# A gated cross-attention and routed-expert kernel: order of the first batches, paced products on GpSimd, and where rows are turned

## The chip, the core and the metric

The kernel runs on one core of one Trainium2 chip. The metric is device time in microseconds (us) of that core, the median of several runs. Engines are called as in the profile: PE (TensorE, with PEld for its weight loads), DVE (VectorE), ACT (ScalarE), POOL (GpSimd) and SP (SyncE, which here only issues transfers). Each runs its own instructions in program order and waits on semaphores for the others.

## The reference

All values are float32. There are 16 batches of 128 rows of 128 features (x) and 77 context rows of 96 features each.

```python
def _layernorm(x, axis=-1, eps=1e-05): ...
# cross-attention: 16 heads of 8
q = (x @ Wq.T + bq).reshape(b, l, h, dh)
kv = (y @ Wkv.T + bkv).reshape(b, m, h, 2 * dh)
k, v = kv[..., :dh], kv[..., dh:]
att = softmax(einsum('blhd,bmhd->blmh', q, k) / sqrt(dh), axis=2)
out = einsum('blmh,bmhd->blhd', att, v).reshape(b, l, d) @ Wo.T + bo
# experts: 4 rounds, 4 experts of 512 hidden features, the best 2 of each row
for r in range(4):
    logits = flat @ Wg[r] + bg[r]
    vals, idx = top_k(logits, 2);  w = softmax(vals)
    cw = sum(one_hot(idx, 4) * w)
    y = einsum('enf,efh->enh', gelu(flat @ W1 + b1), W2) + b2
    cur = cur + einsum('ne,enh->nh', cw, y)
# the whole
x = x + tanh(g_xattn) * xattn(_layernorm(x), ctx)
x = x + tanh(g_ffn) * ffn(_layernorm(x))
```

## The kernel before

**Attention.** The 16 batches are taken one after the other (loop at L1027, "step b"), in four blocks of four. For a block, x is normalized (`stats_x`, `norm_x`, class `Norm` at L236: statistics on DVE, the power -0.5 on POOL at L252, the application on DVE or POOL), turned by PE (`turn_x`), projected to queries (`queries`); the context is turned (`turn_ctx`), and projected to keys and values. `spread_keys` (L744, POOL) multiplies a batch's keys with a mask of heads, so that `scores` (four products into two double banks) gives all heads. `weights` takes the maximum and the difference on DVE and the exponential on ACT; `turn_weights` transposes the exponentials on PE and copies them back on ACT; `attend` sums them and weighs the values on PE, divides on DVE (L820, L822); `put_out` projects. In step b, PE turns the exponentials of b and computes the scores of b+1 in between.

What else has to be done is hung on the steps by hand: the lists `early[b]`, `extra[b]` and `behind[b]` (L908 to L975) hold the turning and projecting of later blocks, the constants of the routing, the gate of the first half and its stores. The order of PE, DVE, ACT and POOL is exactly this program order.

**Start.** SP loads blocks of x and context in turns (L141), ACT's queue the weights (L128 to L133), POOL's queue two bias rows (L137). PE fills its waits with products of a zero tile (`warm`, L664), nine, two, ten, three and four of them. All four batches of the first block are normalized, turned and projected (L844 to L859) before the first scores (L861); the constant rows (`spread_rows`, L867) follow the first exponentials.

**Experts.** The rows are split in two halves h of 1024. In four rounds each half is routed: `gate` ranks the logits, `count`, `route` and `places` find for each row a place, `scatter` (POOL, indirect DMA) stores the rows sorted by their pair of experts into DRAM, `load` (SP) fetches them, `turn_half` transposes them on PE. A phase p (L1111; half p % 2, round p // 2) works through 21 units: eight tiles, five borders, eight tiles. A unit is `first_layer` (four pairs of PE instructions, then gelu on ACT) and, one unit later, `second_layer` (PE, then a sum into the rows on DVE, L1090). `bring` (L991) copies a tile's expert weights on DVE four units ahead (L1000). While one half is in the experts, the other is routed, by the lists `mid[i]` and `post[i]` of the phase.

From round 1 on the logits come without PE: `multiply` (L406, POOL) multiplies the rows with the gate's weights into one of four buffers lp, `sum_up` (L414, DVE) reduces. The products of tiles 0 and 1 are issued in unit 13, 2 and 3 in unit 14, and so on (L1229); each waits for its rows and a free buffer. The last one is issued in unit 0 of the next phase, where also `gate` (unit 1) and `count` (after the first layer of unit 4) stand. In the last round `finish` (L1092) scales a tile and POOL stores it to the output.

**Into the experts.** The first half's stores hang on steps 11 to 14 (L973), its load is issued after step 14 (L1058). After the last step, `turn_half` for the first tiles stands between two groups of four zero products (L1274).

## Time and profile before

| | us |
|---|---|
| median of three runs (467.44 to 468.66) | 467.48 |
| the profiled execution, its own time | 467.39 |
| its span, first to last instruction | 465.6 |
| first scores of batch 0 (sc, L262) start | 18.18 |
| attention product of batch 0 (ps_av) ends | 31.07 |
| first expert product (ps_h) starts | 124.74 |
| PE's last stage (ps_y) ends about | 455.8 |
| last store of the output starts | 457.05 |

How to read it: the page gives busy time by engine, in 40 slices, by group of instructions, and the chain of waits that ended last; the trace behind it can be asked for a timeline, for waits, and for a table of busy time by stage. PEclk is the clock that PE was granted, as a share of full speed. One matmul in float32 shows as two instructions, so four products of a half layer are "x8", 0.89 us apart from start to start at full clock. A wait's cause is the engine or transfer that signalled last. Idle time of an engine that is not the bound costs nothing.

### The profile page before, as it was taken

What the parts mean: (1) busy time and instruction counts of PE and PEld (TensorE: products, weight loads), DVE (VectorE), ACT (ScalarE), POOL (GpSimd) and SP (SyncE); (2) the same over time, 40 slices, a digit from 0 to 9 for tenths busy, and PEclk for the clock granted to TensorE, in tenths of its full rate; (3) what the DMA queues carried; (4) which work ended last, traced back from release to release, by engine and by line L of the source; (5) the groups of instructions that cost most, each with busy time, mean ns of one, the idle gap of its engine ahead of it and who ended that gap; (6) DMA issues with size and microseconds to landing.
All of it is one profiled execution on the core that took longest, in us unless ns stands there. A gap on an engine that the chain in (4) does not pass through costs nothing.

```text
span 465.6 us, 12218 instructions
## 1 busy us (share of the span) xinstructions
PE 445.5 (96%) x4506; PEld 415.4 (89%) x4506; DVE 347.0 (75%) x900; ACT 275.0 (59%) x853; POOL 211.2 (45%) x249
## 2 busy tenths in 40 slices
PE   7999999989899899999999999999999999999991
PEld 6778888777799899999999999999999999999991
DVE  7259998989665998688579768857976885775551
ACT  2356776666555456566656656665665666566560
POOL 5354645227204732582366258236625924461042
PEclk8779999999999989999999999999999999999997
DMA  7420000002201400230121013012101301220000
GB/s 198 137 93 2 4 1 3 2 13 84 95 2 49 139 1 2 72 118 1 48 84 59 1 70 119 1 48 77 67 3 69 118 3 49 94 86 8 1 30 17
DMA packets 19553, 24.08 MB, mean 52 GB/s; under 512 B 3940, under 2 KB 16550, under 8 KB 19366
## 3 DMA queue, kind: packets, MB, share of 16 engines
q1 hardware_dynamic: 14868, 13.41, 9.1%
q0 software_dynamic: 3648, 9.71, 5.7%
q8 instruction: 36, 0.59, 0.5%
q10 hardware_dynamic: 978, 0.18, 0.2%
q14 instruction: 23, 0.19, 0.1%
HBM read 13.58 MB, written 9.71 MB: 50 GB/s over the span
## 4 chain that ended last, share of the span: by engine, by line
PE 81%; issue 7%; DVE 5%; POOL 3%; ACT 2%; POOLq 0%; DVEq 0%; ACTq 0%
PE ps_y L262 28%; PE ps_h L262 28%; PE ps_av L262 6%; PE ps_tr L265 6%; PE sc L262 2%; POOL out_dram L1098 2%; PE ps_warm L262 2%; PE ps_c L265 2%; PE ps_b L262 2%; DVE wb L1000 1%; PE ps_pos L262 1%; PE ps_o L262 1%; ACT exT L800 1%; DVE vm L197 1%; PE ps_q L262 1%
## 5 line engine op out<-in xcount | busy, mean ns | idle before, releaser
L1076 ACT ACTIVATE hT<-ps_h,wb 128x128 f32<-128x128 f32 x512 | 146.0, 368 | 87.9 <-ACT hT L1076 55.4
L262 PE MATMUL ps_h<-curT,wb 128*128 128x128 f32 x1024 | 136.3, 277 | 1.8 <-DVE wb L1000 1.8
L262 PE MATMUL ps_y<-wb,hT 128*128 128x128 f32 x1024 | 136.7, 277 | 0.0
L262 PEld LDWEIGHTS ps_h<-curT,wb 128*128 128x128 f32 x1024 | 125.5, 193 | 2.0 <-DVE wb L1000 2.0
L262 PEld LDWEIGHTS ps_y<-wb,hT 128*128 128x128 f32 x1024 | 125.4, 193 | 0.0
L519 POOL DMA_INDIRECT sorted<-rows,pos_i x64 | 69.6, 1087 | 116.5 <-DVE start L512 61.1
L1000 DVE COPY wb<-wall 128x1028 f32 x128 | 107.5, 842 | 11.7 <-issue 4.0
L93 POOL TENSOR_TENSOR lp<-rows,wg_rows 128x512 f32<-128x512 f32 x48 | 72.5, 1535 | 38.3 <-DVE rows L1090 31.4
L1090 DVE SCALAR_TENSOR_TENSOR rows<-ps_y,pws,rows 128x128 f32<-128x128 f32 x128 | 44.3, 346 | 36.2 <-PE ps_y L262 35.9
L1076 ACT ACTIVATE hT<-ps_h,wall 128x128 f32<-128x128 f32 x160 | 45.6, 368 | 35.9 <-PE ps_h L262 33.8
L800 ACT COPY exT<-ps_tr 77x512 f32<-77x512 f32 x64 | 34.1, 581 | 17.5 <-PE ps_tr L265 17.3
L262 PEld LDWEIGHTS ps_y<-wall,hT 128*128 128x128 f32 x320 | 38.9, 192 | 6.1 <-ACT hT L1076 6.1
L262 PE MATMUL ps_y<-wall,hT 128*128 128x128 f32 x320 | 43.1, 278 | 0.0
L262 PE MATMUL ps_h<-cx,wall 128*128 128x128 f32 x320 | 42.3, 275 | 0.0
L265 PEld LDWEIGHTS ps_tr<-ident,ex 128*77 128x77 f32 x256 | 29.5, 154 | 11.1 <-ACT exT L800 8.3
L262 PEld LDWEIGHTS ps_h<-cx,wall 128*128 128x128 f32 x320 | 39.0, 192 | 0.0
L265 PE MATMUL ps_tr<-ident,ex 128*77 128x128 f32 x256 | 36.8, 289 | 1.7 <-ACT exT L800 1.7
L417 DVE TENSOR_REDUCE lg<-lp 128x4 f32<-128x512 f32 x48 | 32.4, 675 | 5.5 <-POOL lp L93 5.5
L1098 POOL DMA_INDIRECT out_dram<-res,id_i x16 | 18.4, 1151 | 37.0 <-DVE res L1095 36.4
L782 DVE TENSOR_REDUCE mx<-sc 128x8 f32<-128x616 f32 x32 | 25.4, 792 | 11.8 <-PE sc L262 11.7
L792 ACT ACTIVATE ex<-ex 128x616 f32<-128x616 f32 x32 | 23.0, 719 | 10.9 <-DVE ex L786 10.4
L1090 DVE SCALAR_TENSOR_TENSOR rows<-ps_y,pwxs,rows 128x128 f32 x40 | 13.9, 348 | 17.0 <-PE ps_y L262 16.0
(162 smaller groups left out, 463.1 us busy)
## 6 DMA issues: line engine op xcount, KB each, us to landing
rows<-sorted SPq DMA_DIRECT2D x16, 528.0 KB
x_sb<-in_x_dram SPq DMA_DIRECT2D x4, 256.0 KB
wall<-in_L_ffn_W_dram SPq DMA_DIRECT2D x1, 1024.0 KB
wall<-in_L_ffn_W_dram SPq DMA_DIRECT2D x4, 256.0 KB
wg_rows<-wg_turned SPq DMA_DIRECT2D x1, 1024.0 KB
sorted<-rows,pos_i POOLq DMA_INDIRECT x64, 2.5
ctx_sb<-in_ctx_dram SPq DMA_DIRECT2D x4, 115.5 KB
out_dram<-res,id_i POOLq DMA_INDIRECT x16, 2.4
```

The source lines that it names most:

```text
L93: return lambda *a, **kw: tc.keep_in_program_order(f(*a, **kw))
L262: nc.tensor.matmul(*args, **kw)
L265: nc.tensor.transpose(*args)
L417: nc.vector.tensor_reduce(lgs[h][:, t, :], prods.pop((h, t)), AX.X, ALU.add)
L519: ins = nc.gpsimd.indirect_dma_start(out=sorted_rows[h], out_offset=bass.IndirectOffsetOnAxis(ap=pos_i[:, t : t + 1], axis=0), in_=rows[h] ...
L782: beats.append(nc.vector.tensor_reduce(mx, sv, AX.X, ALU.max))
L792: nc.scalar.activation(eu, eu, AF.Exp, scale=1.0 / math.sqrt(DH))
L800: nc.scalar.copy(exT[:, ts(g, HG), :].rearrange("m h l -> m (h l)"), ps[:M, :])
L1000: nc.vector.tensor_copy(wb, wall[:, ds(e, 1), :].rearrange("p o n -> p (o n)"))
L1076: nc.scalar.activation(hT[:, fc, :], ps[:, ts(fc, P)], AF.Gelu_apprx_tanh, bias=wb[:, W_B + fc : W_B + fc + 1],)
L1090: return nc.vector.scalar_tensor_tensor(at, y, w, at, ALU.mult, ALU.add)
L1098: ins = nc.gpsimd.indirect_dma_start(out=out_rows, out_offset=bass.IndirectOffsetOnAxis(ap=id_i[:, t : t + 1], axis=0), in_=res, in_offset ...
```

## The change

It reorders the start, moves single operations between steps and engines, and ties POOL's products to the sums of the units:

- x of batch 0 is loaded alone, then the first context, the two bias rows (now on SP), then the other three batches; bq is loaded into a column of its own.
- Batch 0 alone is normalized, turned and projected before the first scores; the rest of its block follows. Its keys are spread by DVE. The zero products use the banks of the scores: thirteen, one, one and three; the two groups around the last `turn_half` are gone.
- The second zeroed value block and blk are cleared by POOL, after the first scores. The first copy of ACT is a copy of one element.
- The constant rows, the residual of block 0 and the normalization of block 1 hang behind step 0; `turn_x(1)` moves from step 1 to step 2; the bias columns are turned with the constant rows.
- The first half's logits are added ahead of the division of their step; the gate's tanh moves ahead of step 12's exponentials; the stores take four places in step 12 and three in step 13, and the load comes after step 13.
- `turn_half` of the first tiles and the gelu table's first use stand in step 15 ahead of `attend`.
- `multiply` of tile t is issued in unit 13 + t and waits for the sum made in that unit; reductions follow two units later, the last two in units 0 and 1 of the next phase.
- `finish` starts one unit earlier, in another order of tiles.

```diff
@@ -119,26 +119,28 @@
-    NCOL = E * NF + 1
-    cols_n = const.tile([NCOL, P], F32, name="cols_n")
+    cols_n = const.tile([E * NF, P], F32, name="cols_n")
+    bqc = const.tile([P, 1], F32, name="bqc")
...
+    nc.scalar.dma_start(bqc, bq.rearrange("(d o) -> d o", o=1))
     wg_sb = const.tile([D, R, E], F32, name="wg_sb")
...
-    nc.scalar.dma_start(cols_n[E * NF : NCOL, :], bq.rearrange("(o d) -> o d", o=1))
-    nc.scalar.dma_start(cols_n[0 : E * NF, :], b1.rearrange("e (c p) -> (e c) p", p=P))
+    nc.scalar.dma_start(cols_n, b1.rearrange("e (c p) -> (e c) p", p=P))
     bkv_v = bkv.rearrange("(o h t d) -> o t h d", o=1, t=2, d=DH)
...
+    nc.sync.dma_start(x_sb[:, 0, :], x[0])
+    nc.sync.dma_start(ctx_sb[:, 0:BB, :], ctx_768[0:BB].rearrange("b m c -> m b c"))
     for t, w in ((0, wkT), (1, wvT)):
-        gp.dma_start(
-            w[C : C + 1, :].rearrange("o (h d) -> o h d", d=DH), bkv_v[:, t]
-        )
-    for i in range(NB):
+        nc.sync.dma_start(w[C : C + 1, :].rearrange("o (h d) -> o h d", d=DH), bkv_v[:, t])
+    nc.sync.dma_start(x_sb[:, 1:BB, :], x[1:BB].rearrange("b l d -> l b d"))
+    for i in range(1, NB):
         nc.sync.dma_start(
@@ -193,8 +195,7 @@
-    for i in range(2):
-        nc.vector.memset(vm[i], 0.0)
+    nc.vector.memset(vm[0], 0.0)
@@ -208,7 +209,6 @@
-    gp.memset(blk, 0.0)
@@ -403,13 +403,14 @@
-    def multiply(h, r, t):
+    def multiply(h, r, t, behind):
...
-        gp.tensor_tensor(
+        ins = gp.tensor_tensor(
             prods[h, t], rows[h][:, t, 0:D].unsqueeze(1).to_broadcast([P, E, D]), wg_rows[:, r],
...
+        after(ins, behind, "one tile for each piece of work")
@@ -663,29 +664,30 @@
-        ps = bank("ps_warm")
+        ps = banks2("ps_warm")
         for _ in range(n):
-            mm(ps[:, :P], zero, zero, start=True, stop=True)
-    warm(9)
-    ps = bank("ps_wkv")
-    for t in range(2):
-        tp(ps[:C, ts(t, P)], wkv_n[:, t, :], ident)
-    tp(ps[:, 2 * P : 3 * P], wq_n, ident)
-    for t, w in ((0, wkT), (1, wvT)):
-        nc.vector.tensor_copy(
-            w[0:C, :].rearrange("c (h d) -> c h d", d=DH),
-            ps[:C, : 2 * D].rearrange("c (h t d) -> c t h d", t=2, d=DH)[:, t],
-        )
+            mm(ps[:, 0, :P], zero, zero, start=True, stop=True)
+    junk = const.tile([1, 1], F32, name="junk")
+    nc.scalar.copy(junk, zero[0:1, 0:1])
     wqT = const.tile([D, D], F32, name="wqT")
-    nc.scalar.copy(wqT, ps[:, 2 * P : 3 * P])
+    def turn_projections():
+        ps = bank("ps_wkv")
+        for t in range(2):
+            tp(ps[:C, ts(t, P)], wkv_n[:, t, :], ident)
+        tp(ps[:, 2 * P : 3 * P], wq_n, ident)
+        for t, w in ((0, wkT), (1, wvT)):
+            nc.vector.tensor_copy(
+                w[0:C, :].rearrange("c (h d) -> c h d", d=DH),
+                ps[:C, : 2 * D].rearrange("c (h t d) -> c t h d", t=2, d=DH)[:, t],
+            )
+        nc.scalar.copy(wqT, ps[:, 2 * P : 3 * P])
...
-    cols = const.tile([P, NCOL], F32, name="cols")
-    bqc = cols[:, E * NF : NCOL]
@@ -716,17 +718,20 @@
-    def turn_x(i):
+    def turn_x(i, lo=0, hi=BB):
...
-        for j in range(BB):
+        for j in range(lo, hi):
             tp(ps[:, ts(j, P)], row(i * BB + j, 0, D), ident)
+        at = slice(lo * P, hi * P)
         xnTs[i] = awork.tile([P, TB], F32, tag="xnT", name="xnT")
-        nc.scalar.copy(xnTs[i], ps)
-    def queries(i):
+        nc.scalar.copy(xnTs[i][:, at], ps[:, at])
+    def queries(i, lo=0, hi=BB):
         ps = bank("ps_q")
-        mm(ps, wqT, xnTs.pop(i), start=True, stop=True)
-        nc.scalar.activation(qT[i], ps, AF.Identity, bias=bqc)
+        at = slice(lo * P, hi * P)
+        mm(ps[:, at], wqT, xnTs.pop(i)[:, at], start=True, stop=True)
+        nc.scalar.activation(qT[i][:, at], ps[:, at], AF.Identity, bias=bqc)
@@ -741,10 +746,10 @@
-    def spread_keys(b):
+    def spread_keys(b, eng=gp):
...
-        gp.tensor_tensor(
+        eng.tensor_tensor(
             km,
@@ -802,7 +807,6 @@
@@ -816,6 +820,9 @@
+        return ps
+    def over_sums(ps):
         rs = awork.tile([D, L], F32, tag="rs", name="rs")
@@ -826,55 +833,61 @@
-        nc.vector.scalar_tensor_tensor(
+        beats.append(nc.vector.scalar_tensor_tensor(
             row(b, D, D), ps[:, :D], tg[:, 0:1], x_sb[:, b, :],
...
-        )
+        ))
+    warm(13)
+    first_norm, next_norm = Norm(1, "b"), Norm(BB - 1, "c")
+    first_norm.stats(0, x_sb[:, 0, :])
+    first_norm.scale()
+    turn_projections()
     turn_ctx(0)
-    warm(2)
+    warm(1)
+    next_norm.stats(0, x_sb[:, 1, :])
+    first_norm.apply(0, row(0, 0, D), x_sb[:, 0, :], nc.vector)
+    for j in range(1, BB - 1):
+        next_norm.stats(j, x_sb[:, 1 + j, :])
+    next_norm.scale()
+    turn_x(0, 0, 1)
     keys(0)
-    ps = bank("ps_cols")
-    tp(ps[:, :NCOL], cols_n, ident[:NCOL, :NCOL])
-    nc.scalar.copy(cols, ps[:, :NCOL])
-    nc.scalar.copy(
-        wall[:, :, W_B:WW], cols[:, 0 : E * NF].rearrange("p (e c) -> p e c", c=NF)
-    )
-    for j in range(BB):
-        stats_x(0, j)
-    norms[0].scale()
-    kms = {0: spread_keys(0), 1: spread_keys(1)}
+    warm(1)
+    queries(0, 0, 1)
+    warm(3)
+    kms = {0: spread_keys(0, nc.vector), 1: spread_keys(1)}
     stats_x(1, 0)
+    for j in range(1, BB):
+        next_norm.apply(j - 1, row(j, 0, D), x_sb[:, j, :], nc.vector)
     stats_x(1, 1)
-    norm_x(0, nc.vector)
-    stats_x(1, 2)
-    stats_x(1, 3)
-    norms[1].scale()
-    norm_x(1, gp)
-    load_experts()
-    warm(10)
-    turn_x(0)
-    warm(3)
-    queries(0)
-    warm(4)
     scs = scores(0, kms.pop(0))
...
+    gp.memset(vm[1], 0.0)
+    gp.memset(blk, 0.0)
+    load_experts()
+    turn_x(0, 1, BB)
+    queries(0, 1, BB)
     turn_ctx(1)
...
-    keys(1)
...
+        tp(ps[:, 32 : 32 + E * NF], cols_n, ident[: E * NF, : E * NF])
         tp(ps[:, ts(2, D)], wo_n, ident)
...
+        nc.scalar.copy(
+            wall[:, :, W_B:WW],
+            ps[:, 32 : 32 + E * NF].rearrange("p (e c) -> p e c", c=NF),
+        )
         wgT = const.tile([R * E, D], F32, name="wgT")
@@ -907,11 +920,15 @@
+    amid = {b: [] for b in range(B)}
     behind = {b: [] for b in range(B)}
...
-    spread_rows()
-    residual(0)
-    early[1] += [lambda: turn_x(1)]
+    extra[0] += [lambda: keys(1)]
+    behind[0] += [spread_rows, lambda: residual(0)]
+    for j in range(2, BB):
+        behind[0] += [lambda j=j: stats_x(1, j)]
+    behind[0] += [lambda: norms[1].scale(), lambda: norm_x(1, gp)]
+    early[2] += [lambda: turn_x(1)]
     extra[2] += [lambda: queries(1)]
@@ -919,7 +936,7 @@
-            behind[b - 4 + j] += [lambda i=i, j=j: stats_x(i, j)]
+            behind[max(b - 4 + j, 1)] += [lambda i=i, j=j: stats_x(i, j)]
         behind[b - 1] += [lambda i=i: norms[i].scale(), lambda i=i: norm_x(i, gp, (0, 1))]
@@ -945,11 +962,12 @@
-    def gate0(g):
+    def logits0_done(g):
         add_bg(0, 0, g, first["lg"])
-        if g:
-            first["gate"] = gate(0)
-            advance(first["gate"], GATE_1)
+    def gate0():
+        first["gate"] = gate(0)
+        advance(first["gate"], GATE_1)
@@ -965,12 +983,16 @@
-    behind[7] += [lambda: logits0(0), lambda: gate0(0)]
+    amid[7] += [lambda: logits0(0), lambda: logits0_done(0)]
     extra[9] += [lambda: turned0(1)]
-    behind[9] += [lambda: logits0(1), lambda: gate0(1)]
-    behind[10] += [counted0, lambda: advance(first["gate"])]
-    behind[11] += [routed0, placed0, lambda: stored0(0)]
-    stores_at = {(12, 0): 1, (12, 1): 2, (12, 2): 3, (13, 0): 4, (13, 1): 5, (13, 2): 6, (14, 0): 7}
+    amid[9] += [lambda: logits0(1), lambda: logits0_done(1)]
+    behind[9] += [gate0]
+    behind[10] += [counted0, lambda: advance(first["gate"], GATE_2 - GATE_1)]
+    extra[11] += [lambda: advance(first["gate"], 1)]
+    behind[11] += [lambda: advance(first["gate"]), routed0, placed0, lambda: stored0(0)]
+    stores_at = {
+        (12, 0): 1, (12, 1): 2, (12, 2): 3, (12, 3): 4, (13, 0): 5, (13, 1): 6, (13, 2): 7,
+    }
     for b in range(12, 15):
@@ -1019,9 +1041,6 @@
-        junk = const.tile([1, 1], F32, name="junk")
-        nc.scalar.activation(junk, zero[0:1, 0:1], AF.Gelu_apprx_tanh)
@@ -1047,15 +1066,22 @@
-        o[b] = attend(b, exT)
+        if b == B - 1:
+            turn_half(0, 0, state[0]["c"])
+            nc.scalar.activation(junk, zero[0:1, 0:1], AF.Gelu_apprx_tanh)
+        ps_av = attend(b, exT)
+        for f in amid[b]:
+            f()
+        o[b] = over_sums(ps_av)
         for f in behind[b]:
...
-        for k in range(3):
+        for k in range(4):
             if (b, k) in stores_at:
-                scatter(0, first["pos"], stores_at[b, k], stores, beats[n - 3 + k])
-        if b == 14:
+                scatter(0, first["pos"], stores_at[b, k], stores, beats[n - 4 + k])
+        if b == 13:
             load(0, stores)
@@ -1147,7 +1173,10 @@
-                at(post, 0)(lambda: multiply(o, ro, NT - 1))
+                @at(post, 0)
+                def _():
+                    multiply(o, ro, NT - 1, sums[-1])
+                    sum_up(o, NT - 2)
@@ -1226,12 +1255,10 @@
-            for t, i, k in (
-                (0, 13, 14), (1, 13, 15), (2, 14, 16), (3, 14, 17), (4, 15, 18), (5, 17, 19),
-                (6, 19, 20),
-            ):
-                at(post, i)(lambda t=t: multiply(h, r + 1, t))
-                at(post, k)(lambda t=t: sum_up(h, t))
+            for t in range(NT - 1):
+                at(post, 13 + t)(lambda t=t: multiply(h, r + 1, t, sums[-1]))
+                if t < NT - 2:
+                    at(post, 15 + t)(lambda t=t: sum_up(h, t))
@@ -1254,10 +1281,9 @@
-                    if n in (0, 2, 4, 6):
-                        finish(h, n // 2, id_i)
-                    elif n in (1, 3, 5, 7):
-                        finish(h, NT // 2 + n // 2, id_i)
+                    done = {-1: 0, 0: 1, 1: 4, 2: 2, 3: 5, 4: 3, 5: 6, 7: 7}
+                    if n in done:
+                        finish(h, done[n], id_i)
@@ -1271,9 +1297,6 @@
-    warm(4)
-    turn_half(0, 0, state[0]["c"])
-    warm(4)
     for p in range(NHALF * R):
```

## The prediction

> **What bounds the kernel now.** I read the page's busy shares first, then the table of stages (window, length, then busy us and count of PE, weight loads, DVE, ACT, POOL, then PE clock, DMA), because one share over 465.6 us hides stages with different limits.
>
> ```profile
> PE 445.5 (96%) x4506; PEld 415.4 (89%) x4506; DVE 347.0 (75%) x900; ACT 275.0 (59%) x853; POOL 211.2 (45%) x249
> 8.00:12.00 4.00, 3.71 (x16) 2.78 (x17) 3.01 (x14) 0.86 (x4) 2.83 (x4) 0.57 0.76 231
> 12.00:16.00 4.00, 4.00 (x23) 4.00 (x22) 0.00 (x0) 0.42 (x1) 3.76 (x5) 0.58 0.66 208
> 24.00:28.00 4.00, 4.00 (x21) 2.87 (x20) 1.72 (x3) 1.75 (x5) 3.45 (x11) 0.50 0.23 55
> 92.00:99.00 7.00, 5.89 (x101) 4.87 (x99) 5.70 (x16) 4.54 (x12) 0.00 (x0) 1.00 0.01 2
> 121.30:125.00 3.70, 2.97 (x23) 2.54 (x24) 2.00 (x6) 0.58 (x1) 0.00 (x0) 1.00 0.18 62
> 156.00:166.00 10.00, 8.16 (x58) 7.97 (x58) 10.00 (x9) 4.17 (x15) 6.46 (x6) 0.83 0.37 122
> 206.00:247.00 41.00, 41.00 (x363) 40.12 (x362) 32.04 (x88) 25.68 (x92) 21.61 (x17) 1.00 0.16 54
> ```
>
> PE never stops from 166 to 455, so nothing is to be won there, only lost. What can be won lies before 31 (zero products, half clock), at 93 (1.1 idle), at 121 to 125 (zero products and waits) and at 156 to 166. The timeline (start, us, engine, line, operation, idle before, and what ended it) shows these places, and a thing that decides this forecast:
>
> ```profile
> 4.06 0.31 SPq L145 DMA_DIRECT2D ctx_sb<-in_ctx_dram  x1
> ...
> 94.75 1.15 PE L265 MATMUL ps_tr<-ident,ex 128*77 128x128 f32 x8 [1.11 <-ACT exT L800]
> ...
> 155.73 6.04 DVE L1000 COPY wb<-wall 128x1028 f32 x1 [0.35 <-issue]
> 156.27 4.94 POOL L93 TENSOR_TENSOR lp<-rows,wg_rows 128x512 f32<-128x512 f32 x4
> 161.83 1.79 PE L262 MATMUL ps_h<-curT,wb 128*128 128x128 f32 x8 [1.84 <-DVE wb L1000]
> 163.15 0.34 DVE L1090 SCALAR_TENSOR_TENSOR rows<-ps_y,pws,rows 128x128 f32<-128x128 f32 x1
> 163.62 1.27 POOL L93 TENSOR_TENSOR lp<-rows,wg_rows 128x512 f32<-128x512 f32 x1 [2.41 <-issue]
> 164.00 1.44 DVE L1000 COPY wb<-wall 128x1028 f32 x1
> 165.36 0.34 DVE L1090 SCALAR_TENSOR_TENSOR rows<-ps_y,pws,rows 128x128 f32<-128x128 f32 x1
> 166.82 0.34 DVE L1090 SCALAR_TENSOR_TENSOR rows<-ps_y,pws,rows 128x128 f32<-128x128 f32 x1
> 219.44 0.40 DVE L447 TENSOR_TENSOR hot<-rank 128x128 f32<-128x128 f32 x1
> 220.62 0.39 PE L262 MATMUL ps_n<-ones_pp,hot 128*128 128x128 f32 x2
> ```
>
> A weight copy that takes 0.69 alone took 6.04 while POOL ran four products; PE then paused 1.84. Below that: a unit of VectorE (sum, reduce, copy) is 2.21 long (163.15 to 165.36) when a POOL product starts behind the sum, and 1.46 (165.36 to 166.82) when none does. PE needs a unit every 1.79.
>
> **Part 1, the start.** Scores begin at 18.18 now. In the new order:
> - PE: 13 zero products are 26 passes. 18 passes took 4.21 (0.234 each) and PE turned fast about 5.05, so 26 end about 6.0; transposes of the weights and context (0.71 and 0.43) end at 6.9.
> - Loads: SP's queue waits, seen as 1.9 us on wkv_n before the second context load (issued 4.06). The new third bias row and the rest of the first block (192 KB) stand behind such waits, so that load is issued about 4.1. From issue to use, 96 KB took 3.3 and 256 KB 4.2 at most; it lands between 7.0 and 8.4, and I take 7.5. It matters though the first batch doesn't use it: on VectorE its statistics stand ahead of the first batch's normalization, and behind that wait PE's transpose. Blocks 1 to 3 queue behind it on SP; block 1 is first read at about 11.
> - So normalization ends 8.25, transpose 8.5, ACT copy 8.85 (0.27), keys 0.69, queries and three zero products (0.70) end about 10.3; VectorE spreads keys after the 0.42 copy. No row has that op on VectorE: 128x616 took 0.80, 128x128 0.29, so 0.48; POOL's power (1.0) may hold it, 0 to 0.8, I take 0.5. Scores at 10.9, 7.3 earlier.
> - Given back: VectorE has four normalizations and two statistics ahead of the first maximum, and ACT has values (0.75), copy (0.47), queries (0.58), context (0.43) ahead of the first exponential: 15.8 against 21.02. Its transposes start at 16.5 against 23.29, since the constant rows no longer stand before them. PE idles about 1.0 and 1.5 in between, so I give it the half clock that 24 to 28 has now; keys(1) is inside. Attention product 0 ends 24.5 against 31.07: 6.5 gained.
> - Then 2.9 is lost again. The constant rows are now on PE behind it (1.0 at full clock). POOL, in its order: bo_b ready 2.1 after product 0, residual 1.27, power 1.0, normalization of block 1 3.13, constants 1.2, km 0.70, gaps 0.3: keys 3 are spread 9.7 after product 0. PE wants them after rows 1.1, a step 5.44, transposes 1.1 and turn_x 0.5: 8.1. A new wait of 1.6. VectorE's two extra statistics per step: 0.3.
> - Moved and covered: second zero block and blk (2.2 and 0.5 on POOL by the rate of its 128x512 memset, 0.52) run at 11 to 14 before POOL has work, uncovered 0.7; ACT's table load (1.28) is hidden behind the loads; the product and two copies for the bias columns (0.29, 0.18, 0.20) leave the path for the rows' place; the two bias loads leave POOL (0.71 and 0.54), where nothing waits for them; the separate bq load (128 pieces) holds only block 1's load, which has 3 us to spare.
> Start: -3.6 (bounds -1 and -6.5, by the landing and the clock).
>
> **Part 2, gate of the first half.** The tanh no longer holds ACT's copies: PE's 1.1 idle at 93.6 goes, next is VectorE's chain, 0.1 later. Adding the logits ahead of the reciprocal delays a bank at step 10 by 0.2. Together -0.9.
>
> **Part 3, into the experts.** The last store moves from 113.94 to about 109.8, its load from 117.41 to 113.4; the load was used within 5.0 before, so it is there by 118.4, and PE asks at 118.9. Turning costs 0.6 inside step 15 and the first expert product starts at 121.8 instead of 124.74. But oT of batch 15 still comes at 123.4 (VectorE's order, four weight copies first), so ps_o moves from 125.63 to 123.5: -2.1. The gelu table load is covered by attend.
>
> **Part 4, one product per unit.** The pile at 156 goes: 1.84 pause, three half layers at half clock (4.41 for 2.68, so 1.73), 0.28 at ps_n: -3.85. In its place products 2 to 6 each start behind a sum, each unit is 2.21 to 2.24 instead of at most 1.79, and product 7 with a reduce moves into unit 0. Laid out on phase 1: copies and sums slip 0.45 a unit, sum of unit 1 comes at 218.98 instead of 216.35; its reduce, which now waits for POOL until 217.30, starts 219.25; hot ends 1.95 later at 221.8. PE reaches ps_n at 220.62 with 0.78 to spare: it waits 1.25. Weight copies (four ahead) and three ps_y banks still suffice. Five boundaries at 1.25; at the first the products follow the scatter of 155.30 and slip about one more, 2.2. +8.45 (bounds 0 and 12). Behind a waiting product stand only the next products and, from unit 5 on, the scatters, which come later anyway; who waits for it is the copy, and for that the next sum.
>
> The skill says in TensorE: Matmul & The Clock Gate, What's actually happening, that the clock halves after an idle window of about 3.4 us. By that none of my pauses costs more than itself. The rows speak otherwise: PE was cold after 1.84 idle, and at 22 after 0.9, though not after 1.1 at 93.6. By the rows each of six pauses may cost 1.73 more, +10.4. I take no loss, since 1.25 is nearest to the pause that cost nothing, and keep 10.4 for the range. SBUF — State Buffer, SBUF: two separate sides, says whichever of VectorE's two-port op and POOL's op is first holds the shared ports for its instruction. By that the 0.69 copy waits for one product, 1.27; the 6.04 row shows it losing to four in a row. With one product released at a time I use 1.44. It is this rule that makes pacing costly: every product now meets a copy.
>
> **Part 5, the end.** The last store no longer waits for the one before (457.05 to 456.75): -0.3.
>
> **Sum.** -3.6 - 0.9 - 2.1 - 3.85 + 8.45 - 0.3 = -2.3. The profiled execution took 467.39 (span 465.6 and 1.8 around it), 0.09 below the median of 467.48: 465.1, with 462 to 468 for this case.
>
> **Rivals.**
> - Pacing is absorbed: the product yields to the copy, or the slip fits the slack. For it: interleaved units of 1.68 in phase 1 today. Against: the 2.2 units with a gated product. Part 4 is -3.85 alone: 456.7.
> - Slower: the ps_n pause at a phase boundary costs the clock. Place: count of each new phase; price 1.73 each; from three of six boundaries on the time is above 468.9: 470.3 for three, 475.5 for six. For it 0.9 and 1.84 above, against it 93.6.
> - The early start doesn't arrive: the 192 KB load at 8.4, half clock through step 1 and again after the keys wait. Then part 1 is near 0: 468.7. For it: 0.50 clock at 24 to 28 after a short pause.
>
> **How the numbers follow.** Likeliest 0.40, absorbed 0.28, clock lost at boundaries 0.23, start lost 0.09. A measurement tells 0.3% (1.4 us) from no change. Faster: 0.28 and 0.28 of the likeliest; same: 0.11 of it and 0.06 of the last; slower: 0.23, 0.03, 0.01. The range leaves out a tenth on each side: 456.5 to 472.
>
> **What would show it.** Scores near 11, first ex transposes near 16.5; km L93 ending 1.6 behind PE's need in step 2; no 6 us copy; sums 2.2 apart in units 16 to 20; PE idle 1.25 before ps_n in six phases with clock 1.00. It is wrong if sums stay 1.79 apart, if the clock row falls below 0.95 at the boundaries, or if PE is still at half clock beyond 25.

## The result, and the profile after

The changed kernel took 471.91 us (median of 5, 468.42 to 472.3), the kernel before 467.44 beside it: ratio 1.0092, 95% interval 1.0063 to 1.0121. It is 4.5 slower where 2.3 faster was forecast. The profiled execution took 472.17 with a span of 470.2.

The page's busy line, then the table of stages in the windows shown of before (with 99 to 121 added):

```profile
PE 442.2 (94%) x4472; PEld 410.4 (87%) x4472; DVE 362.2 (77%) x901; ACT 277.1 (59%) x855; POOL 205.1 (44%) x248
```

```profile
92.00:99.00 7.00, 6.89 (x108) 5.95 (x109) 6.62 (x21) 4.88 (x13) 0.00 (x0) 1.00 0.01 4
99.00:121.00 22.00, 19.63 (x267) 14.96 (x266) 17.30 (x40) 10.63 (x19) 13.78 (x15) 0.84 0.29 100
156.00:166.00 10.00, 10.00 (x92) 10.00 (x92) 9.48 (x13) 6.48 (x23) 7.13 (x6) 1.00 0.42 135
206.00:247.00 41.00, 39.82 (x350) 38.78 (x349) 33.16 (x86) 24.82 (x87) 18.94 (x17) 1.00 0.17 54
```

The first boundary (156 to 166) is full and at full clock, as forecast. In 206 to 247 PE lacks 1.2 of 41, as forecast for a phase. What the forecast did not look at is 99 to 121: PE's clock is 0.84 there, and PE gets through 267 matmul instructions where the first trace of before has 358 at full clock:

```profile
99.00:121.00 22.00, 20.50 (x358) 16.47 (x357) 20.06 (x50) 14.08 (x24) 13.68 (x15) 1.00 0.24 85
```

The waits of PE in the changed kernel (total, times, longest):

```profile
PE ps_n L262 <- DVE hot L448: 6.6, 6, 1.6
...
PE sc L262 <- POOL km L93: 1.3, 1, 1.3
```

Both were forecast: six waits at ps_n, and km in step 2 (1.6 forecast). The timeline of the start and of the first boundaries:

```profile
9.96 0.85 PE L262 MATMUL sc<-km,qT 32*128 32x308 f32 x8
...
10.15 3.39 DVE L255 TENSOR_SCALAR rows<-x_sb,mvc,rstdc 128x128 f32<-128x128 f32 x3
...
17.00 0.92 PE L265 MATMUL ps_tr<-ident,ex 128*77 128x128 f32 x3 [1.32 <-ACT ex L797]
...
157.22 2.52 POOL L93 TENSOR_TENSOR lp<-rows,wg_rows 128x512 f32<-128x512 f32 x2
157.65 2.65 DVE L1022 COPY wb<-wall 128x1028 f32 x1
...
178.76 0.46 PE L262 MATMUL ps_n<-ones_pp,hot 128*128 128x128 f32 x2 [1.61 <-DVE hot L448]
```

Scores at 9.96 (10.9 forecast), first ex transposes at 17.0 (16.5), the weight copy beside two products 2.65 and no PE pause, then 1.61 before ps_n. And in step 12, the thing not forecast:

```profile
101.24 1.10 PE L262 MATMUL ps_av<-exT,vm 77*32 77x128 f32 x32
...
101.26 1.01 POOL L520 DMA_INDIRECT sorted<-rows,pos_i  x1 [0.17 <-DVE mx L787]
102.28 1.61 PE L265 MATMUL ps_tr<-ident,ex 128*77 128x128 f32 x8
102.58 0.96 POOL L520 DMA_INDIRECT sorted<-rows,pos_i  x1 [0.31 <-DVE mvf L248]
103.85 0.96 POOL L520 DMA_INDIRECT sorted<-rows,pos_i  x1 [0.30 <-issue]
105.69 0.96 DVE L827 RECIPROCAL rs<-ps_av 128x128 f32<-128x128 f32 x1 [2.92 <-PE sc L262]
```

In the first trace of before, rs (the reciprocal of the sums) starts 0.18 behind the end of the same product, with a store of POOL still running:

```profile
103.89 1.10 PE L262 MATMUL ps_av<-exT,vm 77*32 77x128 f32 x32
104.53 0.96 POOL L519 DMA_INDIRECT sorted<-rows,pos_i  x1 [0.30 <-issue]
105.17 0.95 DVE L820 RECIPROCAL rs<-ps_av 128x128 f32<-128x128 f32 x1
```

In the changed kernel the attention product ends at 102.34 by its records, yet VectorE, idle since 102.77, starts rs 3.35 later: PE's signal came late (or the product did; the ends of matmuls are modelled). Eight transposes took 1.61 instead of 1.10. Beside it POOL issues the stores of the first half's sorted rows, three of them behind the start of the product where before has two, since the change put four into this step. I call it the hold. PE's half clock follows at 107.9 to 114.7: steps 12 and 13 take 8.1 and 8.4 instead of 5.4.

Laid beside the first trace of before by the start of ps_av, the change is 3.4 ahead in steps 3 to 7, 2.6 ahead in step 12, 3.2 behind in step 15, 1.1 ahead at the first expert phase's end (178.76 for 179.90), then behind by 1.1 to 1.5 more at each boundary.

### The profile page after: what moved, and what is told of

Same layout as the page of the kernel before. It is cut to its first block, busy times and chain, and to the rows that moved or that the text cites. A ratio compares the mean times of both kernels' runs of the same rounds, so it can differ in the third digit from the quotient of the medians.

```text
span 470.2 us, 12170 instructions
## 1 busy us (share of the span) xinstructions
PE 442.2 (94%) x4472; PEld 410.4 (87%) x4472; DVE 362.2 (77%) x901; ACT 277.1 (59%) x855; POOL 205.1 (44%) x248
## 4 chain that ended last, share of the span: by engine, by line
PE 49%; DVE 20%; issue 16%; POOL 11%; DVEq 1%; ACT 1%; POOLq 0%; ACTq 0%
PE ps_y L262 19%; PE ps_h L262 18%; DVE wb L1022 5%; POOL out_dram L1124 4%; DVE lg L418 3%; POOL rows L93 3%; DVE rows L1116 2%; PE ps_tr L265 2%; PE ps_av L262 2%; PE ps_b L262 2%; POOL km L93 1%; DVE rows L255 1%; PE ps_warm L262 1%; DVEq L999 1%; PE ps_pos L262 1%
## 5 line engine op out<-in xcount | busy, mean ns | idle before, releaser
L1022 DVE COPY wb<-wall 128x1028 f32 x128 | 119.5, 935 | 13.0 <-issue 4.3
L520 POOL DMA_INDIRECT sorted<-rows,pos_i x64 | 70.1, 1096 | 118.6 <-DVE start L513 64.7
L93 POOL TENSOR_TENSOR lp<-rows,wg_rows 128x512 f32<-128x512 f32 x48 | 64.8, 1358 | 48.8 <-DVE rows L1116 38.1
L1116 DVE SCALAR_TENSOR_TENSOR rows<-ps_y,pws,rows 128x128 f32<-128x128 f32 x128 | 44.3, 346 | 35.5 <-PE ps_y L262 34.9
L262 PEld LDWEIGHTS ps_y<-wall,hT 128*128 128x128 f32 x320 | 38.9, 192 | 6.1 <-ACT hT L1102 4.5
L265 PE MATMUL ps_tr<-ident,ex 128*77 128x128 f32 x256 | 38.2, 295 | 4.4 <-ACT exT L805 2.6
L262 PEld LDWEIGHTS ps_h<-cx,wall 128*128 128x128 f32 x320 | 38.9, 192 | 0.0
L791 DVE TENSOR_TENSOR ex<-sc,mx 128x616 f32<-128x616 f32 x32 | 25.5, 796 | 1.4
```

What stands on the lines that cost most here:

```text
L93: return lambda *a, **kw: tc.keep_in_program_order(f(*a, **kw))
L262: nc.tensor.matmul(*args, **kw)
L265: nc.tensor.transpose(*args)
L520: ins = nc.gpsimd.indirect_dma_start(out=sorted_rows[h], out_offset=bass.IndirectOffsetOnAxis(ap=pos_i[:, t : t + 1], axis=0), in_=rows[h] ...
L791: nc.vector.tensor_tensor(eu.rearrange("l (g h) m -> l g h m", h=HG), sv, mx.unsqueeze(3).to_broadcast([P, 2, HG, M]), ALU.subtract,)
L1022: nc.vector.tensor_copy(wb, wall[:, ds(e, 1), :].rearrange("p o n -> p (o n)"))
```

## The experiments

Ratios are to the kernel before on the same chip; one chip's runs stand together under one paragraph where I compare them. "Lag" is rs behind the end of ps_av. Where ps_av itself is stretched beyond its usual 2.0, "held by" counts the stretch and the lag together.

**The changed kernel again, and parts of it undone.** No edit for the first:

> The changed kernel as it is, a second time. Theory A: what the trace shows in attention steps 12 to 14 (PE's signals held for 3.3 us at 102.3, a half-clock window at 107.9 to 114.7, 5.8 us lost against the kernel before) comes from the new places of the stores; then it is there again: 471 to 472.5, with ps_av of step 15 again at about 122. Rival B: it is an accident of single executions; then a second trace has steps 12 to 14 at 5.4 to 6.1 each, ps_av of step 15 at about 116.5, and the median falls to 466 to 468.5. Either way ps_n waits 0.8 to 1.7 in six phases, 6.6 together.

470.65, ratio 1.0093 (1.0071 to 1.0116). The lag in step 12 is 3.2, half clock at 106.3 to 113.1, ps_av of step 15 at 121.7, ps_n waits 6.6. The time is just under the 471 expected, the trace as expected: it is no accident of one execution.

```diff
-                    multiply(o, ro, NT - 1, sums[-1])
-                    sum_up(o, NT - 2)
+                    multiply(o, ro, NT - 1)
...
-            for t in range(NT - 1):
-                at(post, 13 + t)(lambda t=t: multiply(h, r + 1, t, sums[-1]))
-                if t < NT - 2:
-                    at(post, 15 + t)(lambda t=t: sum_up(h, t))
+            for t, i, k in (
+                (0, 13, 14), (1, 13, 15), (2, 14, 16), (3, 14, 17), (4, 15, 18), (5, 17, 19),
+                (6, 19, 20),
+            ):
+                at(post, i)(lambda t=t: multiply(h, r + 1, t))
+                at(post, k)(lambda t=t: sum_up(h, t))
```

> The changed kernel with the logit products and their sums where they were before (part 4 undone). The two traces say that part 4 took 1.8 away at the first phase boundary and added 1.1 to 1.5 at each of five others, 4.3 net: this run is 4.3 below the changed kernel (467.6 from 471.9), the 6 us weight copy and its 1.8 pause are back at the first boundary, and no ps_n waits in the rest. Rival: the ps_n waits are cover for something that comes due just behind them (scatter, load of the next rows); then less than 1.5 is won.

467.07, ratio 1.0009 (0.9994 to 1.0024): pacing costs 0.0084 of 467, 3.9. No ps_n waits; the 6.03 copy and PE's pause of 1.85 are back. As expected.

The next edit puts back the stores' places and the load; with them goes the fourth operation per step that a store may wait for (not shown):

```diff
-        (12, 0): 1, (12, 1): 2, (12, 2): 3, (12, 3): 4, (13, 0): 5, (13, 1): 6, (13, 2): 7,
+        (12, 0): 1, (12, 1): 2, (12, 2): 3, (13, 0): 4, (13, 1): 5, (13, 2): 6, (14, 0): 7,
...
-        if b == 13:
+        if b == 14:
             load(0, stores)
```

> The changed kernel with the stores of the first half's rows again three to a step (steps 12 and 13, the last in 14) and their load in step 14. Theory A (the four stores in step 12 hold PE's signals): the hold and the half clock of steps 12 to 14 go, 5.8 less, and up to 2 is lost again because the load comes a step later and the turning in step 15 waits for it: 466 to 468. Rival B (accident): like the second run of the changed kernel, or up to 2 more.

471.92, ratio 1.0144 (1.0123 to 1.0166), a miss. The lag in step 12 fell to 1.9 and no half clock follows it, as Theory A says; but the price of the later load was more than "up to 2": from step 14 to the first count of the experts this trace takes 25.4, the changed kernel beside it 21.3.

```profile
117.38 0.93 SPq L537 DMA_DIRECT2D rows<-sorted  x2
121.11 0.42 PEld L265 LDWEIGHTS ps_c<-ident,rows 128*128 128x128 f32 x4 [1.95 <-DMA rows<-sorted]
```

PE waits 1.76 at the turning in step 15, and the half clock comes there, at 122.0 to 128.9. The old order of logits, tanh and counts in steps 7 to 11 in addition:

```diff
-    amid[7] += [lambda: logits0(0), lambda: logits0_done(0)]
+    behind[7] += [lambda: logits0(0), lambda: gate0(0)]
...
-    amid[9] += [lambda: logits0(1), lambda: logits0_done(1)]
-    behind[9] += [gate0]
-    behind[10] += [counted0, lambda: advance(first["gate"], GATE_2 - GATE_1)]
-    extra[11] += [lambda: advance(first["gate"], 1)]
-    behind[11] += [lambda: advance(first["gate"]), routed0, placed0, lambda: stored0(0)]
+    behind[9] += [lambda: logits0(1), lambda: gate0(1)]
+    behind[10] += [counted0, lambda: advance(first["gate"])]
+    behind[11] += [routed0, placed0, lambda: stored0(0)]
```

> As the kernel with the old stores, and the gate of the first half (logits, tanh, counts, steps 7 to 11) in its old order as well. Steps 8 to 11 took 0.7 more than before by the trace, not 0.9 less as forecast. If the new order itself costs that, this is 0.7 below the kernel with the old stores; if the order gains 0.9 and something else in those steps costs 1.6, it is 0.9 above it, with PE's wait for the exT copy behind the tanh back at about 1.1.

472.19, ratio 1.0146 (1.0108 to 1.0184): within the noise of the kernel with the old stores. But its trace has steps 7 to 12 in 33.22 against 33.90 there, so the new order costs 0.7; every other trace with the old order takes 33.2 there, every one with the new order 33.9. The reason stands in the changed kernel's step 7 (VectorE's rows):

```profile
69.40 0.18 DVE L397 TENSOR_TENSOR lg<-ps_lg,rows_b 128x16 f32<-128x16 f32 x1 [1.21 <-PE ps_lg L262]
69.50 0.95 DVE L827 RECIPROCAL rs<-ps_av 128x128 f32<-128x128 f32 x1
```

The add of the logits, now ahead of the reciprocal, waits 1.21 for PE; reciprocal, statistics, POOL's power and the normalization behind it come 1.0 later, and the turned rows of step 8 wait. The 1.1 behind the tanh did go, and 0.9 of new waits (0.40 and 0.48) stand in its place.

**What holds PE.** Ten one-column zero products in PE's wait for km:

```diff
-    early[2] += [lambda: turn_x(1)]
+    early[2] += [lambda: turn_x(1), lambda: pad(10)]
```

> The changed kernel with ten one-column zero products (40 PE instructions) put into PE's wait for km in step 2, so that PE's later instructions stand about where they stood in the kernel before (ps_av of step 12 at instruction 2616, 2614 before, 2576 changed). In steps 12 and 13 of the changed kernel PE's instructions come in bundles some 0.7 apart though they wait for nothing. Theory C: this hangs on where a stretch of 128 small instructions lies in PE's instruction stream; then the hold after ps_av of step 12 (rs 3.3 behind it) and the half clock behind it are gone or elsewhere, 4 to 6 faster than the changed kernel. Rival D: it comes from the stores on POOL beside it; then rs stays 2 or more behind ps_av in step 12 and the time is that of the changed kernel within 1.

469.84, ratio 1.0058 (1.0029 to 1.0087). Lag 3.37 in step 12, half clock at 107.7: theory C falls. Nor is it a fetch of instructions under way: by the DMA records the changed kernel's trace has none from 97.0 to 108.0, this one has one in the hold (102.9 to 104.6), and the lags are equal. The time is 1.6 lower than the changed kernel's ratio gives, where within 1 was expected; this trace gains 2.2 at the first phase boundary, which comes up below. Stores 1 to 7 in steps 14 and 15, load and turning behind:

```diff
-        (12, 0): 1, (12, 1): 2, (12, 2): 3, (12, 3): 4, (13, 0): 5, (13, 1): 6, (13, 2): 7,
+        (14, 0): 1, (14, 1): 2, (14, 2): 3, (14, 3): 4, (15, 0): 5, (15, 1): 6, (15, 2): 7,
...
-            turn_half(0, 0, state[0]["c"])
...
-        if b == 13:
+        if b == 15:
             load(0, stores)
...
+    turn_half(0, 0, state[0]["c"])
     for p in range(NHALF * R):
```

> The changed kernel with stores 1 to 7 of the first half's rows moved from steps 12 and 13 to 14 and 15, their load behind step 15 and the turning for the first expert product behind the loop. Rival D (stores hold PE): steps 12 and 13 take 5.4 to 6.1 each with rs within 1 of ps_av, and the hold shows in step 14 or 15. Theory C (place in the stream): steps 12 and 13 still show it. In all about 5 slower at the start of the experts, since the load then stands in the open; the time itself tells nothing.

481.25 (ratio 1.0301, 1.0265 to 1.0337). Step 12 is free and step 13 takes 6.0 (lag 1.34), the hold went with the stores:

```profile
102.30 0.95 DVE L827 RECIPROCAL rs<-ps_av 128x128 f32<-128x128 f32 x1
...
114.46 0.96 POOL L520 DMA_INDIRECT sorted<-rows,pos_i  x1 [0.30 <-issue]
115.73 0.96 POOL L520 DMA_INDIRECT sorted<-rows,pos_i  x1 [0.30 <-issue]
117.53 0.96 DVE L827 RECIPROCAL rs<-ps_av 128x128 f32<-128x128 f32 x1 [3.24 <-remote]
```

A lag of 0.27 in step 12, and 3.96 in step 14 beside four stores. PE waited 8.6 for the rows' load, and half clock follows from 117.7 to 138.2: by the ratios this kernel is 9.8 above the changed one, where about 5 was expected.

The kernel before, with no edit, as one execution on that chip:

> The kernel before, for a second trace: under both theories steps 12 to 14 take 5.4 to 6.1 each with rs within 1 of the end of ps_av, as in the first; if the hold shows here too, it is no part of the change.

A miss: 464.88, and held in step 12 too. Its ps_av takes 3.48 where 2.0 is usual, in bundles of a few instructions 0.75 apart. So the hold is no invention of the change; the change makes it longer. And this execution has only 0.06 of half clock in its first 31 us, where the first trace had 0.22: the start of the kernel before is not one number.

**Pacing only where the pile was.**

```diff
+            if p == 0:
+                for t in range(NT - 1):
+                    at(post, 13 + t)(lambda t=t: multiply(h, r + 1, t, sums[-1]))
...
+            else:
+                for t, i, k in (
+                    (0, 13, 14), (1, 13, 15), (2, 14, 16), (3, 14, 17), (4, 15, 18), (5, 17, 19),
+                    (6, 19, 20),
+                ):
+                    at(post, i)(lambda t=t: multiply(h, r + 1, t))
+                    at(post, k)(lambda t=t: sum_up(h, t))
```

> The changed kernel with the products of the later phases where they were before, and only those of phase 0 one for each piece of work. By the traces pacing wins 1.8 at the first boundary and loses 1.1 to 1.5 at each later one: this is 1.5 to 2 below the kernel with all products in the old places and about 6 below the changed kernel. Rival: what the pile at the first boundary cost comes back as the ps_n wait of 1.6 there; then it is within 0.5 of the kernel with the old products.

464.09, ratio 0.9939 (0.9922 to 0.9957), faster than both kernels, and by more than expected: 0.0070 (3.3) below the undone pacing, 1.5 to 2 expected. PE waits once for ps_n in this trace, at the first boundary:

```profile
PE ps_n L262 <- DVE hot L449: 1.6, 1, 1.6
```

From there to its last product the trace takes 275.9, the changed kernel's 282.0: five waits and their slip cost 6.2.

The first boundary is not one number either. From the first count to the second, eight traces paced in phase 0 take 41.0 with the wait at ps_n; five (padded, late_stores, the old stores and two below) take 38.9 without it. In those the copy starts before the product that is released beside it, the product waits 0.4, and a unit is 1.69 long; in the others the product starts first and the unit is 2.2. The padded kernel's rows:

```profile
158.58 0.68 DVE L1027 COPY wb<-wall 128x1028 f32 x1
158.74 10.07 POOL L93 TENSOR_TENSOR lp<-rows,wg_rows 128x512 f32<-128x512 f32 x6 [0.90 <-DVE rows L1121]
160.04 0.91 DVE L1027 COPY wb<-wall 128x1028 f32 x1
161.72 0.91 DVE L1027 COPY wb<-wall 128x1028 f32 x1
```

This is the forecast's rival "absorbed", come true at this boundary in some executions. How often it does so was not measured; it may be why the time is lower than expected.

**The start alone, and with the old tail.** The first undoes all but the new start; the second keeps the start, pacing in phase 0 and the new finish, with gate, stores and turning as before. To both, beside the edits of gate and stores shown above:

```diff
+        nc.scalar.activation(junk, zero[0:1, 0:1], AF.Gelu_apprx_tanh)
...
     extra[B - 1] += [begin]
...
-        if b == B - 1:
-            turn_half(0, 0, state[0]["c"])
-
-            nc.scalar.activation(junk, zero[0:1, 0:1], AF.Gelu_apprx_tanh)
...
+    warm_m(4)
+    turn_half(0, 0, state[0]["c"])
+    warm_m(4)
     for p in range(NHALF * R):
```

The first has the products of the undone pacing above besides, the second those paced in phase 0.

> The kernel before with the new start alone (gate, stores, turning, products and finish as before). The changed kernel's trace reaches step 3 at 43.15, the first trace of the kernel before at 46.52 with two half-clock windows ahead of it (13.7 us), its second at 42.74 with one of 3.4. If the start gains what its own order saves (3.4, as forecast 3.6), this is 3 to 3.5 faster than the kernel before; if most of it was only the clock of one execution, 0 to 1.5.

463.39, ratio 0.9980 (0.9966 to 0.9995), 0.9 faster: the second of the two cases, not the 3.6 of the forecast.

> New start, products of phase 0 one for each piece of work and those of the later phases where they were, new finish; gate, stores (three to a step) and turning as before. If four stores in a row cost the changed kernel the hold (3.3) and the half-clock window (3.4) behind it, and the turning in step 15 saves 2.5, this is 2 to 4 below the version that had the same products with the new gate and stores (464.1 beside 467.0 for the kernel before), so about 5 below the kernel before, and 2 below the new start alone. If the three stores to a step bring the same hold and window here, it is no faster than that version.

460.56, ratio 0.9917 (0.9887 to 0.9946). On this chip no trace was held (lags of 0.2 to 0.8 in steps 12 to 14), so the fall from 0.9980 is pacing in phase 0 and the finish: 2.9. Below the kernel with the new gate, stores and turning (0.9939, on another chip) it is 1.0, where 2 to 4 was expected: by this those three together cost little.

To the kernel paced in phase 0, eight stores of spare rows into a scratch tensor, four in step 5 and four in step 6:

```diff
+    def spare_store(t):
+        ins = nc.gpsimd.indirect_dma_start(
+            out=scratch,
+            out_offset=bass.IndirectOffsetOnAxis(ap=num_p[:, t : t + 1], axis=0),
+            in_=blk[:, 0:RW],
+            in_offset=None,
+        )
+        after(ins, beats[-1], "now")
...
+    for b in (4, 5):
+        behind[b] += [lambda b=b, t=t: spare_store((b - 4) * 4 + t) for t in range(4)]
```

> The version with only phase 0 paced, and eight more indirect stores of 128 rows to a scratch tensor, four behind step 4 and four behind step 5, where the trace shows no hold. Their traffic and POOL time are extra work. If POOL's stores in a row hold PE's small instructions, rs stands 2 or more behind ps_av in step 5 or 6 (0.1 to 0.2 now) and PE's instructions come in bundles there; if steps 12 and 13 are special for another reason, steps 5 and 6 keep rs within 0.5 and only km may come late.

Steps 5 and 6 keep lags of 0.21 and 0.07. What came late was POOL's own work behind the stores: PE waited 1.67 for km and four times, 3.2 in all, for rows that POOL normalizes, a half-clock window followed at 68.7, and the two steps took 7.5 more. But steps 12 and 13, with their four stores, had 0.28 and 0.82 too, so on this chip it says nothing on what holds PE. Inconclusive.

The same eight as plain stores on SP's queue:

```diff
-        ins = nc.gpsimd.indirect_dma_start(
-            out=scratch,
-            out_offset=bass.IndirectOffsetOnAxis(ap=num_p[:, t : t + 1], axis=0),
-            in_=blk[:, 0:RW],
-            in_offset=None,
-        )
+        ins = nc.sync.dma_start(scratch[t * P : (t + 1) * P, :], blk[:, 0:RW])
```

> The same with eight plain DMA stores of the same 128 rows each from SP's queue in place of the indirect ones. If the traffic to memory is what holds PE, steps 5 and 6 show the hold here too; if it is POOL's issuing of indirect stores, they stay as in the version with phase 0 paced (rs within 0.5 of ps_av).

Likewise unheld and inconclusive on its question, but it shows the new tail without a hold:

```profile
115.36 0.92 SPq L538 DMA_DIRECT2D rows<-sorted  x2
119.13 0.72 PEld L265 LDWEIGHTS ps_c<-ident,rows 128*128 128x128 f32 x4 [2.21 <-DMA rows<-sorted]
```

PE asks for the rows at 117.1, they land at 119.1, and the half clock follows at 118.6 to 128.9. The count of phase 0 comes at 138.54, with the old tail on the same chip at 134.56. In the trace with the indirect stores, where everything from step 6 on comes later, PE finds the rows there.

**Four stores or three, on a chip that holds.** The changed kernel once more:

> The changed kernel a third time, beside kernels with the old tail on the same chip. If the hold belongs to its four stores in a row, rs is again 3.2 to 3.4 behind ps_av in step 12 and the half clock comes at about 107. If it belongs to the chip, steps 12 to 14 take 5.4 to 5.6; then the turning in step 15 asks for the rows at about 117, before their load has landed (about 119), and waits 2 with a half-clock window behind it, as in the version with extra plain stores. Either way 4 to 5 above the kernel before.

470.68, ratio 1.0080 (1.0062 to 1.0098). Lag 3.34 in step 12, half clock at 108.9.

The old tail once more:

> The old tail again: 3 to 5 below the kernel before. Held in step 12 by 1 to 2 if the chip is one that holds, then about 3 below; not held, about 4 below.

463.09, ratio 0.9922 (0.9894 to 0.9950), held in step 12 by 1.5, no half clock. The profile's bundles:

```profile
101.09 0.96 POOL L521 DMA_INDIRECT sorted<-rows,pos_i  x1 [0.30 <-issue]
...
101.83 0.42 PE L262 MATMUL ps_av<-exT,vm 77*32 77x128 f32 x3 [0.31 <-issue]
102.58 0.44 PE L262 MATMUL ps_av<-exT,vm 77*32 77x128 f32 x6 [0.33 <-issue]
...
103.06 0.96 DVE L828 RECIPROCAL rs<-ps_av 128x128 f32<-128x128 f32 x1 [1.30 <-PE ps_av L262]
```

"issue" means that PE waited for nothing the profile shows; products that start 0.03 apart on average otherwise come three and six at a time, 0.75 apart.

The old tail with the changed kernel's stores and load (and the fourth operation per step that a store may wait for, not shown):

```diff
-        (12, 0): 1, (12, 1): 2, (12, 2): 3, (13, 0): 4, (13, 1): 5, (13, 2): 6, (14, 0): 7,
+        (12, 0): 1, (12, 1): 2, (12, 2): 3, (12, 3): 4, (13, 0): 5, (13, 1): 6, (13, 2): 7,
...
-        if b == 14:
+        if b == 13:
             load(0, stores)
```

> The old tail (old gate order, turning behind step 15 with zero products around it), but stores four to a step and their load in step 13 as in the change. If four stores in a row make the hold, step 12 has rs 3 behind ps_av and it is 3 to 6 above the old tail beside it; if the turning in step 15 was what cost, it is within 1 of the old tail, or up to 2 below since the load lands earlier.

464.36, ratio 0.9964 (0.9945 to 0.9984). Stages 99 to 121 of the old tail, then of this one:

```profile
99.00:121.00 22.00, 19.90 (x334) 15.14 (x335) 18.86 (x45) 12.57 (x22) 12.44 (x14) 1.00 0.29 100
```

```profile
99.00:121.00 22.00, 18.26 (x278) 13.61 (x281) 16.19 (x40) 11.06 (x19) 12.01 (x14) 0.92 0.29 98
```

With the fourth store in the step the hold grows from 1.5 to 2.8, a half-clock window comes (103.2 to 106.6), and from step 12 to step 15 the trace takes 21.61 against 18.83. By the times this costs 0.0042 of 466, 2.0 (0.4 to 3.6 by the two intervals); by the traces 2.8. Both lie between the two cases expected (3 to 6, or within 1). The edit moves the load too, so the 2.0 is the price of both.

One thing holds in all 13 held traces, with two stores behind the start of ps_av, with three and with four: rs starts 0.70 to 1.03 behind the end of the last of these stores (104.81 and 105.69 in the changed kernel, 116.69 and 117.53 with the late stores, 102.05 and 103.06 with the old tail). In the five traces that are not held it starts 0.3 to 0.8 before that end. One store more, 0.96 and the 0.30 before it, is 1.3 more of hold.

The kernel before on the same chip:

> A third trace of the kernel before: held in step 12 by 1 to 2 if the chip holds, not at all otherwise; in both cases less than the changed kernel beside it.

468.53; step 12 held by 1.5, as on that chip the old tail. Its first phase boundary has the same pause as the first trace of before, no half clock behind it, and a wait at ps_n instead:

```profile
162.97 1.16 PE L262 MATMUL ps_h<-curT,wb 128*128 128x128 f32 x8 [1.84 <-DVE wb L1000]
181.04 0.46 PE L262 MATMUL ps_n<-ones_pp,hot 128*128 128x128 f32 x2 [1.65 <-DVE hot L447]
```

## Why the prediction was wrong, step by step

- **Start, forecast -3.6, measured -0.9.** The layout was right: scores, transposes and the end of the first attention product (24.87 for 24.5) came as laid out, and 3.4 was gained on the trace it was laid out against. The mis-sized term is that trace. The first 31 us of the three traces of before and of the changed kernel:

```profile
0.00:31.00 31.00, 26.64 (x188) 21.34 (x188) 15.95 (x40) 10.63 (x25) 15.23 (x49) 0.78 0.55 160
0.00:31.00 31.00, 26.35 (x218) 21.42 (x218) 19.69 (x46) 12.89 (x30) 16.41 (x53) 0.94 0.53 160
0.00:31.00 31.00, 26.75 (x200) 22.18 (x200) 17.42 (x43) 11.19 (x27) 15.29 (x49) 0.83 0.55 160
0.00:31.00 31.00, 25.25 (x240) 20.21 (x244) 21.14 (x48) 13.94 (x32) 11.13 (x22) 0.89 0.49 142
```

The clock there was 0.78, 0.94 and 0.83 before (6.8, 1.7 and 5.1 lost); with the new start it was 0.89 (3.4 lost) in all traces but one. Step 3 begins at 46.52, 42.74 and 45.15 before, and at 42.4 to 44.3 (mean 43.3) in the 15 traces with the new start. Less the clock's loss that is 39.7 to 41.0 before and 38.9 to 41.3 after: what the order itself saves can't be told from nothing by these traces. The forecast counted one execution's half clock as if it were always there.
- **Gate, forecast -0.9, measured +0.7.** "Adding the logits ahead of the reciprocal delays a bank at step 10 by 0.2" failed: the add waits 1.21 for PE in step 7, and everything behind it on VectorE and POOL moves.
- **Stores, forecast nothing, measured +2.0 (by traces +2.8).** Part 3 priced the earlier stores only by what they freed, and put nothing for what POOL's stores do to PE beside them; no row of the first trace spoke against it. The load did not come at 113.4 either but at 115.0, and so can come late for the turning.
- **Turning, forecast -2.1, about -2.4** where PE was held: from ps_av of step 12 to the count of phase 0 the changed kernel takes 36.95 on the last chip, the kernel with four stores and the old turning 39.37. Where PE is not held the two traces differ: in one the rows are there and it takes 32.18 (34.03 with the old tail), in the other the gain turns into a wait of 2.0 and half clock, 37.88.
- **Pacing, forecast -3.85 + 8.45 = +4.6, measured +3.9** (4.3 in the two traces). Five boundaries at 1.25 each forecast, 1.1 to 1.5 found: this step held. The first boundary, -1.65 forecast and -1.83 in the traces (ps_n from 42.87 behind the first count to 41.04), came out near for the wrong reason. The 1.73 of half clock in the -3.85 was not on the path: without it the third trace of before takes 42.88, since PE then waits 1.65 for VectorE's hot. And 41.04 is one of two outcomes, 38.9 the other. No clock was lost at any of the six pauses in the profiled execution, though the longest was 1.61; in the second trace a window of 3.4 follows that one.
- **End, -0.3, measured -0.4** (9.44 from PE's last product to the end, 9.84 before).

The measured terms add to 2.9 to 4.1 of the 4.5; they come from different chips, and the rest is within their intervals. So the steps that failed are the start's size, the gate's sign and the stores' missing price; that pacing costs more than it gains was in the forecast. Forecast and rivals shared the error: the rival that ended slower put the clock's loss at the phase boundaries, and its size (470.3 with three windows) is near 471.9 by chance. TensorE: Matmul & The Clock Gate in the Trainium skill, What's actually happening, has the clock halve after an idle window of some 3.4 us. The traces here don't agree: of the 36 half-clock stretches in the clock records of all traces ahead of 440 us, 35 begin where PE's records have no idle stretch above 2.1 in the 3.4 before, and the one of step 13 follows 1.1. But the forecast's reading of its rows, that a pause such as 1.84 costs the clock, doesn't hold either: of four traces with that pause at the first boundary three have a window behind it and one has none.

**Open.** Why PE is held beside POOL's stores on three chips and not on a fourth; the chip of the first trace of before, which is not held, is not on record. It issues its stores at the same places in step 12 as the two held traces of the same program. That the stores are needed is shown (the hold moved with them), and that more of them in a row make it longer; what of a store PE shares is not. Neither the place in PE's stream nor, on the one chip where it was tried, extra stores in other steps brought it about.

## What to carry to other kernels

Before a stage is laid out against a trace, look at the clock in that stage in more than one execution; a half-clock window that comes and goes (1.7 to 6.8 lost here) is worth as much as most edits. An operation moved "off the path" onto another engine is priced by what that engine does to its neighbours, and here indirect stores in a row slowed a stream of small matmuls. A fix that removes a pile at one place should be applied at that place: paced in the first phase alone it won, in all phases it lost; with the start and the old tail it makes the best version, 0.992 of the kernel before.

## What was not expected of the hardware

PE's small matmuls came in bundles 0.75 apart, and its signals to VectorE and ScalarE up to 4 us late, while POOL issued indirect stores of 0.96 to 1.24 each, and came free 0.7 to 1.0 after the last of them; on one of four chips nothing of it was seen. A weight copy of 0.69 took 2.65 beside two POOL products in a row and 6.04 beside four, and 1.39 to 1.49 beside one that had started before it; where the copy had started first it took 0.68 to 0.91 and the product 1.7 instead of 1.3.
